# A weight matrix for each of the two dense blocks of a graph-attention layer, and the second block started three slots after the first

## The chip, the cores and the metric

The kernel runs on one core of one Trainium2 chip. A core has five engines that work through queues of their own: TensorE (PE in the profile; its weight loads are listed as PEld), VectorE (DVE), ScalarE (ACT), GpSimd (POOL) and SyncE (SP, which here only starts transfers). They meet through semaphores. The on-chip memory has 128 partitions; TensorE writes its products into a separate accumulator memory (PSUM). Transfers between the device's main memory and the on-chip memory run on 16 DMA engines that all queues share.

The metric is device time in microseconds (us) of one execution of the whole program; lower is better. The kernel before has a median of 2652.23 us over nine runs (2638.36 to 2659.0).

## The reference

One block of a graph network over 6250 nodes with 256 features and 100,000 edges, sorted by destination. Destinations are drawn with a square law, so that the low-numbered nodes have by far the most edges.

```python
xn = layernorm(x)
# graph layer 1 (GCN), with self loops
h1 = relu(segment_sum((xn @ W1)[src] * dinv[src] * dinv[dst], dst) + b1)
# graph layer 2 (GAT)
xw = h1 @ W2
e  = leaky_relu((xw @ a_src)[src] + (xw @ a_dst)[dst], 0.2)
p  = exp(e - segment_max(e, dst)[dst])
h2 = relu(segment_sum(p[:, None] * xw[src], dst) / segment_sum(p, dst) + b2)
x  = x + h2 + mix(xn)              # mix: linear attention with normed k and v
x  = x + experts(layernorm(x))     # two of eight experts a node, gelu between
```

The change lies in the second graph layer (the lines of `e`, `p` and `h2`).

## The kernel before, in words

Nodes are cut into 49 blocks of 128 (`NB = 49`, `P = 128`). The edges of a block of destinations are packed into tiles of 128 edges. For 47 of the blocks a tile's source rows are fetched from a table in main memory (`ftab`: 256 features, a one, the source's score and its parts, 260 numbers a row) by an indirect DMA of GpSimd, one gather for 128 rows, and are added up by TensorE with a matrix that has the edge's weight at (edge, destination). The first two blocks (`ND = 2`) have so many edges that they are done densely: `many[:, b, :, :]` holds how many edges run from each of the 6272 (padded) sources to each of the 128 destinations of block b, and the attention weight is worked out for every pair, in a matrix `W` of 128 x 49 x 128 numbers (24.5 KB a partition). TensorE then multiplies it with all of `ftab`, which is streamed through in 14 transfers of 900 KB (seven for each block) into two buffers `F`.

The second layer is written as a plan over slots. A slot is a third or a half of a chunk (8 to 12 tiles of one block). A chunk that begins at slot s is announced at s - 12, gathered from s - 14, its scores transposed, looked up and turned into weights by s - 1, and added up from slot s on. Slots before 0 are the start-up; the dense blocks are planned into them. For every slot the loop runs the lists `loads`, `early`, then the aggregation `add_up2` (line 1932), then `tensor`, then `late` and `last`. The order of TensorE, ScalarE, VectorE and GpSimd is exactly the order in which the loop issues; only SyncE's transfers are ordered by the scheduler. Every engine takes its instructions in order, so that one that waits holds up all behind it.

The gathered rows go into a ring of 75 rows. Its first 48 lie in the tile `xres`, the last 27 (`NR2 = 27`) in a tile of their own, `ring2` (named `ring` in the profile). A row can be filled again once TensorE has added up the tile that was in it. At the start all rows are empty, so that the first 75 gathers can run ahead.

The steps of a dense block b that is planned at slot s, by their lines in the kernel before:

- s, `seen`, lines 1993 (ScalarE) and 1994 (VectorE), seven times each: which sources are seen, and their scores, into W.
- s + 1, `tops`, line 1998 (VectorE): the maximum over the sources; s + 2, transposed by TensorE (2002), and `maxima` (2006 to 2015, VectorE, small).
- s + 3, `in_rows`, line 2019 (TensorE): the destinations' scores and maxima in rows.
- s + 4, `plus`, line 2022, and `leaky`, line 2027 (VectorE): the score and the leaky relu.
- s + 5, `minus`, line 2030 (VectorE), and `powers_of`, line 2041 (ScalarE): minus the maximum, and the exponential.
- s + 6, `times`, line 2045 (VectorE): times the number of edges.
- s + 7, `through`, line 2051 (TensorE): 49 matmuls with the streamed `F` (line 2036 starts the transfers).
- s + 8, `dense_taken`, line 2061 (VectorE): the block itself is added, into `dacc`.

In the kernel before the first block has s = -14 and the second s = -7, and both use the one W. After the second layer's slots the rest of the experts' work follows; part of it runs within the slots.

Of the kernel before, what the change touches and what calls it, by code (L numbers as in the profile page):

```python
# [9 lines left out]
FP = mybir.dt.float32  # L10
# [4 lines left out]
AF = mybir.ActivationFunctionType  # L15
ALU = mybir.AluOpType
AX = mybir.AxisListType
# [7 lines left out]
P = 128  # L25
# [9 lines left out]
def graph_block(  # L35
# [22 lines left out]
    nc = tc.nc  # L58
# [6 lines left out]
    NB = (N + P - 1) // P  # L65
# [36 lines left out]
    ND, GD, MOST = 2, 8, 2048  # L102
    GPB, HS = P // GD, 7
# [13 lines left out]
    GW = D + 4  # L117
# [55 lines left out]
    with ExitStack() as s0:  # L173
# [170 lines left out]
        for i in range(NB):  # L344
            st = e2.tile([P, 6], FP, name="st")
# [1024 lines left out]
    def roomy():  # L1370
# [14 lines left out]
        with ExitStack() as s1:  # L1385
# [116 lines left out]
        with ExitStack() as s2:  # L1502
# [24 lines left out]
            for b in range(ND, NB):  # L1527
# [186 lines left out]
        with ExitStack() as s3:  # L1714
# [30 lines left out]
            NR1, NR2 = NB * RW // GW, 27  # L1745
            NR3 = NR1 + NR2
            ring1 = xres.rearrange("p i d -> p (i d)")[:, : NR1 * GW].rearrange("p (i d) -> p i d", d=GW)
            ring2 = rp.tile([P, NR2, GW], FP, name="ring")
# [7 lines left out]
            GO = 14  # L1756
# [198 lines left out]
            def at(plan, s, what, *of):  # L1955
                plan.setdefault(s, []).append((what, of))

            for ch in chunks:
                s, n = ch["at"], len(ch["cut"]) - 1
# [22 lines left out]
                    at(late, s + n + 1, end, ch)  # L1982

            dm = tc.alloc_tile_pool(name="dm", bufs=1, side="right")
            W = dm.tile([P, NB, P], FP, name="W")
            pshares = ex.take()
            nc.scalar.copy(pshares[:, :NB], share[:, :, 0])
            shares = pshares[:, :NB, None]

            def seen(b, h0):  # L1990

                hs = slice(h0, h0 + HS)
                nc.scalar.activation(W[:, hs, :], many[:, b, hs, :], AF.Identity, bias=lowest, scale=BIG)
                nc.vector.tensor_tensor(W[:, hs, :], W[:, hs, :], shares[:, hs].to_broadcast([P, HS, P]), op=ALU.min)

            def tops(st):
                st["mx"] = mx = dm.tile([P, P], FP, name="mx")
                nc.vector.tensor_reduce(mx, W.rearrange("p h d -> p d h"), AX.X, ALU.max)

            def tops_turned(st):  # L2000
                st["pt"] = pt = ex.take()
# [17 lines left out]
                nc.tensor.matmul(pr, ones, st["diag"].rearrange("p j d -> p (j d)"), start=True, stop=True)  # L2019

            def plus(st):
                nc.vector.tensor_tensor(W, W, st["pr"][:, None, :P].to_broadcast([P, NB, P]), op=ALU.add)

            def leaky():
                for h0 in range(0, NB, HS):
                    part = W[:, h0 : h0 + HS, :]
                    nc.vector.scalar_tensor_tensor(part, part, 0.2, part, op0=ALU.mult, op1=ALU.max)

            def minus(st):
                nc.vector.tensor_tensor(W, W, st["pr"][:, None, P:].to_broadcast([P, NB, P]), op=ALU.subtract)  # L2030
                ex.give(st["pr"])
                nc.scalar.activation(st["keep"], st["keep"], AF.Exp)

# [3 lines left out]
                    F, ftab[h0 * P : (h0 + HS) * P, 0 : D + 1].rearrange("(h p) d -> p h d", p=P)  # L2037
                )

            def powers_of(h0):  # L2040
                nc.scalar.activation(W[:, h0 : h0 + HS, :], W[:, h0 : h0 + HS, :], AF.Exp)

            def times(b, h0):
                hs = slice(h0, h0 + HS)
                nc.vector.tensor_tensor(W[:, hs, :], W[:, hs, :], many[:, b, hs, :], op=ALU.mult)

            def through(st, h0):
                if h0 == 0:
                    st["pa"] = ps3.tile([P, D + 1], FP, name="agg", bufs=2)
                for h in range(h0, h0 + HS):  # L2050
                    nc.tensor.matmul(
                        st["pa"], W[:, h, :], st["F", h0][:, h - h0, :], start=(h == 0), stop=(h == NB - 1)
                    )

            def dense_own(b, st):
# [20 lines left out]
            nc.vector.tensor_scalar(lowest, lift, -1.0, None, op0=ALU.mult)  # L2076
            parts7 = range(0, NB, HS)
            for b in range(ND):
                st, s = {}, -GO + 7 * b
                for h0 in parts7:  # L2080
                    at(late, s, seen, b, h0)
                at(late, s + 1, tops, st)
                at(tensor, s + 2, tops_turned, st)
                at(late, s + 2, maxima, b, st)
                at(tensor, s + 3, in_rows, st)
                at(late, s + 4, plus, st)
                at(late, s + 4, leaky)
                at(late, s + 5, minus, st)
                at(loads, s + 2, dense_own, b, st)
                for n, h0 in enumerate(parts7):  # L2090
                    at(loads, s + 4 + n // 3, stream, st, h0)
                    at(last, s + 5, powers_of, h0)
                    at(late, s + 6, times, b, h0)
                    at(tensor, s + 7, through, st, h0)
                at(late, s + 8, dense_taken, b, st)
                at(loads, 3, dense_mixed, b, st)
                at(late, 4 + b, dense_end, b, st)
# [59 lines left out]
```

## Time and profile before

| what | value |
|---|---|
| median of nine runs | 2652.23 us (2638.36 to 2659.0) |
| profiled execution, its own time | 2645.85 us |
| its span | 2644.1 us |
| busy: PE, DVE, ACT, POOL | 1978.0, 1473.6, 756.6, 1593.2 us |
| start-up of the second layer (first `seen` to first regular aggregation after the dense blocks) | about 1149 to 1312 us |
| its regular slots | about 1312 to 2275 us |
| the experts' rest | about 2275 to 2644 us |

The page gives busy time by engine, the span in 40 slices, and the costliest groups of instructions. In a list in order of time a row has start, duration, engine, line, operation, what it writes and reads, its shape and how many instructions are merged; in brackets stands how long the engine was idle ahead of it, and what ended the wait. "issue" means that nothing the profile shows was waited for. A matmul of 32-bit numbers appears as two passes, so 49 matmuls are 98 passes. `x7` marks seven instructions merged into one row. The granted clock of TensorE is given as a share of full speed.

### The profile page before, as it was taken

The page shows a single profiled execution, that of the slowest core. Times are in us where ns is not written, and L with a number is a line of the kernel's source. Part 1 is how long each engine was busy: PE and PEld are TensorE (multiplying, and loading weights), DVE is VectorE, ACT ScalarE, POOL GpSimd, SP SyncE. Part 2 cuts the span into 40 slices and gives each one's busy share as a digit, 9 for nine tenths or more (in the row PEclk, how much of TensorE's full clock was granted, in tenths as well). Part 3 has the DMA queues.
Part 4 walks back from the last instruction along what each step waited for, and adds up shares of the span by engine and source line. Part 5 has one row for each costly group of instructions (what it writes and reads, how often), then busy time and mean ns, then how long its engine had stood idle before and what let it go on. Part 6 is the DMA issues. An engine that isn't in the chain of part 4 may idle for free. (4 is left out here: it accounts for less than half of the span.)

```text
span 2644.1 us, 34183 instructions
## 1 busy us (share of the span) xinstructions
PE 1978.0 (75%) x9261; PEld 1465.0 (55%) x9261; DVE 1473.6 (56%) x5122; ACT 756.6 (29%) x1914; POOL 1593.2 (60%) x1753
## 2 busy tenths in 40 slices
PE   3478888888889987734677679989998797688600
PEld 2355555555556666623445457767776585576500
DVE  6422454554534424476598676888776676531332
ACT  3242112232332200012233234544544353211100
POOL 1106777777777767747177777777777774100076
PEclk9698898988999989967799789999998898799855
DMA  4254344444447567746355576777676665364366
GB/s 135 56 189 149 114 119 120 122 122 121 126 131 225 161 207 221 219 137 209 115 172 165 148 232 204 224 238 228 210 241 210 212 192 160 100 231 151 119 200 177
DMA packets 299243, 450.28 MB, mean 170 GB/s; under 512 B 44666, under 2 KB 225566, under 8 KB 298879
## 3 DMA queue, kind: packets, MB, share of 16 engines
q0 software_dynamic: 77184, 210.12, 27.9%
q1 hardware_dynamic: 209710, 226.65, 26.8%
q10 hardware_dynamic: 12145, 11.19, 1.4%
q8 instruction: 78, 1.28, 0.2%
q14 instruction: 126, 1.03, 0.1%
HBM read 377.19 MB, written 71.40 MB: 170 GB/s over the span
## 5 line engine op out<-in xcount | busy, mean ns | idle before, releaser
L1576 POOL DMA_INDIRECT xres<-ytab,srcidx x698 | 688.8, 987 | 304.0 <-DMA wr<-in_L_mix_w_qkv_dram 82.8
L1798 POOL DMA_INDIRECT xres<-ftab,srcidx x455 | 450.3, 990 | 210.6 <-PE agg L1932 82.1
L1580 PE MATMUL agg<-xres,S 128*128 128x256 f32 x1396 | 380.9, 410 | 70.0 <-DMA xres<-ytab,srcidx 68.4
L1580 PEld LDWEIGHTS agg<-xres,S 128*128 128x128 f32 x1396 | 265.4, 200 | 181.1 <-DMA xres<-ytab,srcidx 126.8
L1798 POOL DMA_INDIRECT ring<-ftab,srcidx x243 | 237.6, 978 | 74.1 <-issue 27.1
L1932 PE MATMUL agg<-xres,PW 128*128 128x257 f32 x910 | 248.1, 415 | 11.8 <-ACT PW L1925 11.8
L880 PE MATMUL px<-xT,w1q 128*128 128x256 f32 x896 | 231.1, 410 | 29.2 <-DVE xT L868 14.9
L1925 ACT ACTIVATE PW<-S,z 128x128 f32<-128x128 bf16 x698 | 224.5, 392 | 98.9 <-DVE S L1908 32.3
L956 POOL DMA_INDIRECT yg<-ys,part x98 | 96.7, 987 | 229.3 <-issue 215.0
L880 PEld LDWEIGHTS px<-xT,w1q 128*128 128x128 f32 x896 | 175.7, 204 | 63.2 <-DVE xT L868 18.1
L902 PE MATMUL px<-w2q,hT 128*128 128x256 f32 x896 | 208.1, 383 | 1.1 <-DVE yb L907 1.0
L434 DVE TENSOR_REDUCE var<-sq 128x16 f32<-128x1024 f32 x49 | 59.8, 1220 | 260.6 <-ACT sq L432 260.6
L1932 PEld LDWEIGHTS agg<-xres,PW 128*128 128x128 f32 x910 | 180.4, 206 | 41.0 <-ACT PW L1925 12.8
L427 PE MATMUL kv<-wkvT,xnT 128*128 128x512 f32 x392 | 182.2, 608 | 8.8 <-DVE vv L446 8.8
L902 PEld LDWEIGHTS px<-w2q,hT 128*128 128x128 f32 x896 | 166.5, 190 | 25.3 <-DVE yb L907 1.4
L887 ACT ACTIVATE hT<-px,b1T 128x256 f32<-128x256 f32 x224 | 96.1, 472 | 231.3 <-PE px L880 194.9
L784 POOL DMA_INDIRECT xs<-xn,to_i x98 | 99.9, 1019 | 101.5 <-DVE slot L761 63.0
L907 DVE TENSOR_TENSOR yb<-px,fb 128x256 f32<-128x256 f32 x112 | 44.7, 421 | 198.0 <-PE px L902 170.1
L1932 PE MATMUL agg<-ring,PW 128*128 128x257 f32 x486 | 133.0, 416 | 0.0
L427 PEld LDWEIGHTS kv<-wkvT,xnT 128*128 128x128 f32 x392 | 76.0, 199 | 88.5 <-issue 74.3
L1844 DVE TENSOR_REDUCE mt<-pm 128x1 f32<-128x384 f32 (+1 forms) x201 | 122.2, 608 | 1.5 <-PE pm L1837 1.5
L1908 DVE TENSOR_TENSOR S<-iota_b,dlc 128x384 bf16<-128x384 bf16 (+1 forms) x201 | 122.9, 612 | 0.0
(359 smaller groups left out, 3210.3 us busy)
## 6 DMA issues: line engine op xcount, KB each, us to landing
w1q<-in_L_ffn_W_dram SPq DMA_DIRECT2D x56, 512.0 KB
w2q<-in_L_ffn_W_dram SPq DMA_DIRECT2D x56, 512.0 KB
xg<-xs SPq DMA_DIRECT2D x56, 256.0 KB
ys<-yb SPq DMA_DIRECT2D x56, 256.0 KB
F<-ftab SPq DMA_DIRECT2D x14, 899.5 KB
Y<-ytab SPq DMA_DIRECT2D x14, 896.0 KB
xnT<-xnTd SPq DMA_DIRECT2D x98, 128.0 KB
xres<-ytab,srcidx POOLq DMA_INDIRECT x698
```

Of the source, the lines that this page charges most:

```text
L427: nc.tensor.matmul(kv[:, s, :], xnT[:, k, :], wkvT[:, k, s * INNER : (s + 1) * INNER], start=(k == 0), stop=(k == 1),)
L784: put = nc.gpsimd.indirect_dma_start(out=xs[:, :], out_offset=bass.IndirectOffsetOnAxis(ap=to_i[:n, j, k : k + 1], axis=0), in_=bt["xn"][k ...
L880: nc.tensor.matmul(ph, w1q[:, k, c * P : (c + 1) * P], xT[:, k, :], start=(k == 0), stop=(k == 1))
L902: nc.tensor.matmul(py, hT[:, c, j * P : (j + 1) * P], w2q[:, c, :], start=(c == 0), stop=(c == HC - 1))
L956: back = nc.gpsimd.indirect_dma_start(out=yg[:n, :], out_offset=None, in_=ys[:, :], in_offset=bass.IndirectOffsetOnAxis(ap=self.slot[:n, j ...
L1576: nc.gpsimd.indirect_dma_start(out=R, out_offset=None, in_=ytab[:, :], in_offset=bass.IndirectOffsetOnAxis(ap=srcidx[:, t : t + 1], axis=0),)
L1580: nc.tensor.matmul(sums[b], hot[s][:, t - t0, :], R, start=(t == first[b]), stop=(t == first[b + 1] - 1))
L1798: nc.gpsimd.indirect_dma_start(out=ch["R"][c], out_offset=None, in_=ftab[:, :], in_offset=bass.IndirectOffsetOnAxis(ap=srcidx[:, ch["t0"] ...
L1844: nc.vector.tensor_reduce(ch["mt"][:, q : q + 1], ch["pm", q][:, :w, :].rearrange("p c e -> p (c e)"), AX.X, ALU.max)
L1908: nc.vector.tensor_tensor(S[:, : c1 - c0], iota_b[:, None, :].to_broadcast([P, c1 - c0, P]), dlc[:, t0 + c0 : t0 + c1, None].to_broadcast( ...
L1925: nc.scalar.mul(PW[:, c - c0, :], ch["S", q][:, c - c0, :], ch["z"][:, c : c + 1])
L1932: nc.tensor.matmul(ch["pa"], ch["PW", q][:, c - c0, :], ch["R"][c][:, 0 : D + 1], start=(c == 0), stop=(c == ch["C"] - 1),)
```

## The change

Each dense block has a weight matrix of its own. The first block's is laid over the first 6272 of the 7020 numbers (a partition) of the ring's last 27 rows, `ring2`; the second block's is the tile `W` that was there. The ring's gathers into those rows follow in the program behind the first block's use of them. The second block is planned three slots behind the first (s = -11) and no longer seven (s = -7). The steps, their operations and their shapes are the same; the functions take the block's state `st`, from which they read its matrix.

```diff
             dm = tc.alloc_tile_pool(name="dm", bufs=1, side="right")
-            W = dm.tile([P, NB, P], FP, name="W")
+
+            assert NR2 * GW >= NB * P and ND == 2
+            Ws = [
+                ring2.rearrange("p i d -> p (i d)")[:, : NB * P].rearrange("p (h d) -> p h d", d=P),
+                dm.tile([P, NB, P], FP, name="W"),
+            ]
...
-            def seen(b, h0):
-
-                hs = slice(h0, h0 + HS)
+            def seen(b, st, h0):
+
+                W, hs = st["W"], slice(h0, h0 + HS)
...
             def plus(st):
-                nc.vector.tensor_tensor(W, W, st["pr"][:, None, :P].to_broadcast([P, NB, P]), op=ALU.add)
-
-            def leaky():
+                nc.vector.tensor_tensor(st["W"], st["W"], st["pr"][:, None, :P].to_broadcast([P, NB, P]), op=ALU.add)
+
+            def leaky(st):
                 for h0 in range(0, NB, HS):
-                    part = W[:, h0 : h0 + HS, :]
+                    part = st["W"][:, h0 : h0 + HS, :]
                     nc.vector.scalar_tensor_tensor(part, part, 0.2, part, op0=ALU.mult, op1=ALU.max)
...
                 for h in range(h0, h0 + HS):
                     nc.tensor.matmul(
-                        st["pa"], W[:, h, :], st["F", h0][:, h - h0, :], start=(h == 0), stop=(h == NB - 1)
+                        st["pa"], st["W"][:, h, :], st["F", h0][:, h - h0, :], start=(h == 0), stop=(h == NB - 1)
                     )
...
             for b in range(ND):
-                st, s = {}, -GO + 7 * b
+                st, s = {"W": Ws[b]}, -GO + 3 * b
                 for h0 in parts7:
-                    at(late, s, seen, b, h0)
+                    at(late, s, seen, b, st, h0)
                 at(late, s + 1, tops, st)
...
                 at(late, s + 4, plus, st)
-                at(late, s + 4, leaky)
+                at(late, s + 4, leaky, st)
                 at(late, s + 5, minus, st)
```

`tops`, `minus`, `powers_of` and `times` read `st["W"]` in the same way.

More of the change, by code (lines that the diff above doesn't have):

```diff
@@ L1997, in tops @@
                 st["mx"] = mx = dm.tile([P, P], FP, name="mx")
-                nc.vector.tensor_reduce(mx, W.rearrange("p h d -> p d h"), AX.X, ALU.max)
+                nc.vector.tensor_reduce(mx, st["W"].rearrange("p h d -> p d h"), AX.X, ALU.max)
             def tops_turned(st):
@@ L2021, in plus @@
             def plus(st):
-                nc.vector.tensor_tensor(W, W, st["pr"][:, None, :P].to_broadcast([P, NB, P]), op=ALU.add)
-            def leaky():
+                nc.vector.tensor_tensor(st["W"], st["W"], st["pr"][:, None, :P].to_broadcast([P, NB, P]), op=ALU.add)
+            def leaky(st):
                 for h0 in range(0, NB, HS):
-                    part = W[:, h0 : h0 + HS, :]
+                    part = st["W"][:, h0 : h0 + HS, :]
                     nc.vector.scalar_tensor_tensor(part, part, 0.2, part, op0=ALU.mult, op1=ALU.max)
             def minus(st):
-                nc.vector.tensor_tensor(W, W, st["pr"][:, None, P:].to_broadcast([P, NB, P]), op=ALU.subtract)
+                nc.vector.tensor_tensor(st["W"], st["W"], st["pr"][:, None, P:].to_broadcast([P, NB, P]), op=ALU.subtract)
                 ex.give(st["pr"])
@@ L2038, in stream, with powers_of, times @@
                 )
[L2040 to L2044, printed above, removed]
+            def powers_of(st, h0):
+                part = st["W"][:, h0 : h0 + HS, :]
+                nc.scalar.activation(part, part, AF.Exp)
+            def times(b, st, h0):
+                W, hs = st["W"], slice(h0, h0 + HS)
                 nc.vector.tensor_tensor(W[:, hs, :], W[:, hs, :], many[:, b, hs, :], op=ALU.mult)
@@ L2091, in roomy @@
                     at(loads, s + 4 + n // 3, stream, st, h0)
-                    at(last, s + 5, powers_of, h0)
-                    at(late, s + 6, times, b, h0)
+                    at(last, s + 5, powers_of, st, h0)
+                    at(late, s + 6, times, b, st, h0)
                     at(tensor, s + 7, through, st, h0)
```

## The prediction

> **What bounds the kernel now.** I read the page first (shares, slices, costliest groups), then the busy time by stage, then GpSimd's, VectorE's and TensorE's instructions in order of time around the start of the second layer, and last the waits.
>
> Lines of the costliest groups: all of the second layer's gathers are issued by GpSimd at line 1798, 455 + 243 = 698 of them.
>
> ```profile
> L1798 POOL DMA_INDIRECT xres<-ftab,srcidx x455 | 450.3, 990 | 210.6 <-PE agg L1932 82.1
> L1798 POOL DMA_INDIRECT ring<-ftab,srcidx x243 | 237.6, 978 | 74.1 <-issue 27.1
> ```
>
> Busy time by stage (columns: PE, PEld, DVE, ACT, POOL with instruction counts, granted clock, DMA share, GB/s):
>
> ```profile
> 1250.00:1270.00 20.00, 1.20 (x6) 0.44 (x5) 19.97 (x11) 0.00 (x0) 1.86 (x2) 0.50 0.08 20
> 1290.00:1310.00 20.00, 16.18 (x59) 12.94 (x58) 0.00 (x0) 0.00 (x0) 0.00 (x0) 0.83 0.54 162
> 1500.00:1600.00 100.00, 79.09 (x439) 61.47 (x436) 66.61 (x283) 39.68 (x120) 76.23 (x79) 0.86 0.65 203
> 1800.00:1900.00 100.00, 94.65 (x541) 75.00 (x540) 82.90 (x342) 47.60 (x143) 76.18 (x79) 0.95 0.76 241
> ```
>
> From 1400 to 2200 us GpSimd does 78 or 79 instructions in every 100 us, whatever the others do. In its list one gather starts 1.253 us after the last (0.95 busy, 0.30 between), and 100/1.253 is 79.8: it is saturated, so it paces the layer. From 1312.8 us to its last gather (2223.1) no idle of more than 0.31 us stands before a gather. The two long ones are earlier:
>
> ```profile
> 1251.22 0.95 POOL L1798 DMA_INDIRECT ring<-ftab,srcidx  x1 [0.31 <-issue]
> 1278.28 2.91 POOL L1798 DMA_INDIRECT xres<-ftab,srcidx  x1 [26.11 <-PE agg L1932]
> 1312.80 1.11 POOL L1798 DMA_INDIRECT xres<-ftab,srcidx  x1 [27.60 <-PE agg L1932]
> ```
>
> The ring has 75 rows. At 1252 us all are full, and gather 76 needs the first aggregation (line 1932) to free a row. That comes late because VectorE and TensorE are still at the dense blocks:
>
> ```profile
> 1157.21 10.62 DVE L1998 TENSOR_REDUCE mx<-W 128x128 f32<-128x6272 f32 x1
> 1228.93 1.09 DVE L1994 TENSOR_TENSOR W<-W,px 128x896 f32<-128x896 f32 x1 [3.81 <-ACT W L1993]
> 1232.53 10.62 DVE L1998 TENSOR_REDUCE mx<-W 128x128 f32<-128x6272 f32 x1
> 1263.73 6.68 DVE L2030 TENSOR_TENSOR W<-W,px 128x6272 f32<-128x6272 f32 x1
> 1312.13 0.48 DVE L2061 SCALAR_TENSOR_TENSOR dacc<-own,dkeep,agg 128x257 f32<-128x257 f32 x1 [28.54 <-PE agg L2051]
> ```
>
> Block 1's first pass (line 1994) creeps from 1200.9 to 1230.0 us because each seventh of the one W is rewritten only after block 0's products have read it; its other passes follow only then. TensorE's products (line 2051) themselves wait for F:
>
> ```profile
> 1194.02 8.24 PE L2051 MATMUL agg<-F,W 128*128 128x257 f32 x28 [6.29 <-DVE W L2045]
> 1224.54 3.28 PE L2051 MATMUL agg<-F,W 128*128 128x257 f32 x14 [1.62 <-DMA F<-ftab]
> 1280.62 6.36 PE L2051 MATMUL agg<-F,W 128*128 128x257 f32 x28
> 1308.81 3.28 PE L2051 MATMUL agg<-F,W 128*128 128x257 f32 x14 [1.88 <-DMA F<-ftab]
> ```
>
> Block 0's products take 1194.0 to 1227.8 = 33.8 us, block 1's 1280.6 to 1312.1 = 31.5 us: 4.8 and 4.5 us per seventh, against 3.28 for a seventh's matmuls at full clock. So: what the change is worth is how much earlier gather 80 starts (1312.80 now), since from it on GpSimd runs without a pause.
>
> **The change part by part.** All durations are from the profiled execution (2645.85 us, span 2644.1), 6.4 us under the median of the nine runs (2652.23); I apply the difference to the median.
>
> *Nothing is added or removed.* The same passes, matmuls, 14 F loads and gathers run; only places in the queues change. Two places are checked for a new wait below.
>
> *VectorE's chain to block 0's products.* By the built order block 1's first pass (7.1) and its maximum (10.62) now stand between block 0's steps. Up to 1169.7 (diagonals of block 0) nothing moves. Then: first pass of block 1 7.1, to 1176.8 (its ScalarE half no longer waits for products; the 1.31 wait for line 2019 is hidden beneath it); line 2022 6.7, to 1183.5; line 2027 7.1, to 1190.6; block 1's maximum 10.6, to 1201.2; Q 0.4 and line 2030 6.7, to 1208.3; block 1's small steps 1.3, to 1209.6; first seventh of line 2045 1.1, to 1210.7. TensorE must first do block 1's row product (1.22) and a pm group (0.59 + 0.60) after 1209.6, so block 0's products start at 1212.1, not 1194.0: 18.1 us later. With 33.8 us they end at 1245.9.
>
> *Block 1's chain.* Lines 2022 and 2027 of block 1 (13.8) run beneath block 0's products, 1218 to 1232. But line 2030 of block 1 stands behind block 0's dacc (line 2061) on VectorE, so it waits for 1245.9: dacc 0.5 and line 2030 6.7, to 1253.1; then 2.2 to TensorE's first matmul (before: line 2030 ended 1191.9, products began 1194.0), so 1255.3. Queued behind dacc are also the pm reduction that TensorE needs ahead of the products (0.55, beneath the exponential) and Q of the third chunk, for which SP's dq load stands ahead of four F loads: Q ends near 1262, when the F buffer of the second seventh is read (1255.3 + 6.4), so SP loses about nothing. Block 1's first two F come as block 0's last buffers free (1241 and 1246) and land before 1255.3, as they were ahead at 1280.6 before. With 31.5 us the products end at 1286.8, not 1312.1.
>
> A row bounds this span from the other side: the 33.8 of block 0, whose first 28 matmuls took 8.24 at granted clock 0.5 instead of 6.36. TensorE will have done little for 9 us before. The Trainium skill, "TensorE: Matmul & The Clock Gate" (What's actually happening), has the clock fall to half after an idle window of about 3.4 us; the 8.24 after an idle of 6.29 agrees, and by that rule the sum below would be about 2 us worse.
>
> *From there to a free row.* Now slots -3 to -1 stand between. dacc 0.5 and the one-hot S 0.7 to 1288.0; pm reduction 0.55 and a pm group 0.8 on TensorE to 1289.3, beneath which ScalarE's four scalings run (1.27); a row is free 1.5 after the aggregation starts (1276.78 to 1278.28): gather 76 at 1290.8, gather 80 four periods (5.0) later, 1295.8. Ends: 0.7 for all of it (1312.1 to 1312.80 before), or 4 us more if the slots' small steps do not overlap, and 2 more if gather 76 again lasts 2.91.
>
> *Ring rows hold block 0's W.* The built order shows each of gathers 49 to 72 now waiting for TensorE on its own. Row r needs W's columns up to about 2.03(r + 1); with block 0's sevenths read from 1212.1 to 1245.9, row 9 is free at 1227 (nominal start 1229.9), row 23 at 1246 (1247.5): nearly no wait. Even if all 27 waited for 1245.9 they would end 27 x 1.253 = 33.8 us later, at 1279.7, still 11 us under gather 76. I take nothing. The cover is gone if block 0's products end after 1257.
>
> *After gather 80.* Everything is paced by GpSimd. ScalarE still waits 24.0 us for gathers at the very end:
>
> ```profile
> 2214.98 0.23 ACT L1808 COPY a<-xres 128x44 bf16<-128x44 bf16 x1 [16.17 <-DMA xres<-ftab,srcidx]
> 2226.03 0.23 ACT L1808 COPY a<-xres 128x44 bf16<-128x44 bf16 x1 [7.83 <-DMA xres<-ftab,srcidx]
> ```
>
> so the shift reaches the end of the layer, and the experts behind it hold the same work in the same order.
>
> Sum: 1312.8 - 1295.8 = 17.0 us. Ends: 17.0 + 3.0 = 20 (gather 76 0.7 after the products), and 17.0 - 2.3 - 4 - 2 = 8.7. I take 17.0: its terms are rows of this very stretch. Profiled: 2628.9; against the median: 2635.
>
> **The rivals.**
> *The loads get dearer (slower).* The F loads share the DMA engines with the gathers: from 1210 to 1230 their busy share is 0.96 at 293 GB/s. With A and B the two product spans, gather 80 starts at 1230.5 + A + B; it breaks even at A + B = 82.3, or 5.9 us per seventh for all 14, and is 0.3% slower from 6.5. The dearest row is the F load issued at 1202.3 whose matmuls started at 1210.5 (8.2). At 6.6 per seventh, 10 us slower: 2662. For it: that share. Against: block 0's 4.8 were already beside gathers, and they end near 1255 as before, so block 1's are not. In the Trainium skill, "DMA: Bandwidth & Descriptors" (Issuing engines are not separate DMA queues) says that queues of different engines do not bring separate DMA engines; 293 GB/s with both streams against 162 with F alone shows that one stream alone left room here.
>
> *The gain is swallowed (same).* TensorE is 94% busy from 1800 to 2000 us, and there ScalarE hardly waits for gathers; were TensorE the true pacer with GpSimd only keeping up, an earlier start would be lost in between: 2652. Against: before 1600 ScalarE waits for gathers over and over (some 80 us from 1400 to 1600), and again at the end, so TensorE's own work would start earlier too.
>
> *More is saved.* If F were always there in time for block 1, its products would take 7 x 3.28 = 23 us, 8.5 less: 2627. Against: two buffers, and a load of about 5 us (issued 1283.96, used 1288.98).
>
> **How the numbers follow.** Forecast 0.72 (2632 to 2644 by its own ends), more saved 0.06, swallowed 0.12, dearer loads 0.10. What a measurement of this kernel can tell from no change is about 0.3%, 8 us; all of the forecast lies beyond it. So faster 0.78, same 0.12, slower 0.10. The nine runs spread over 21 us, so a median may be off by some 3. The range takes in most of "more saved" and half of "swallowed": 2626 to 2651.
>
> **What would show it.** After: block 1's first pass in one piece at about 1170; block 0's products from 1212 to 1246; dacc of block 0 with a wait of some 12 us ahead of it; block 1's products from 1255 to 1287; one long idle before gather 76, ending near 1291, in place of 26.1 and 27.6; no other above 3 us; last gather near 2206. Wrong if the products' spans sum to over 70 us, if a gather after 76 waits for TensorE again, or if the last gather is early but the span is not.

## The result and the profile after

The changed kernel takes **2629.13 us** (median of ten runs, 2622.86 to 2637.31), the kernel before beside it 2651.87 us (31 runs, 2638.36 to 2659.3). The ratio is 0.9918, with a 95% interval of 0.9903 to 0.9933: 22.7 us by the medians. The forecast was 2635 us, in a range from 2626 to 2651.

The profiled execution of the changed kernel is not a typical one: 2640.6 us (span 2638.8), 11.5 us above its median. The excess lies ahead of everything that the change touches: the dense blocks' first pass on VectorE (line 1999, `seen`, 1994 before) starts at 1161.67 us, in the profile before at 1150.10, and in a second profile of the changed kernel, which lies at its median, at 1153.12. All offsets below are therefore counted from that pass in each profile. "Gather n" is the n-th of the second layer's gathers (line 1798); the two columns of the changed kernel are its first profile and the one of a second group of runs. In the lists, rows that lie between those shown are left out.

| us after the first dense pass | before | forecast | after | after, again |
|---|---|---|---|---|
| block 0's products | 43.9 to 77.7 | 62.0 to 95.8 | 61.5 to 94.9 | 61.4 to 96.7 |
| block 1's products | 130.5 to 162.0 | 105.2 to 136.7 | 104.2 to 134.9 | 106.0 to 136.1 |
| gather 76 | 128.2 | 140.7 | 138.1 | 139.3 |
| gather 80 | 162.7 | 145.7 | 143.3 | 144.5 |
| last gather | 1073.0 | 1055.9 | 1058.4 | 1055.2 |
| from gather 80 to the end of the span | 1331.3 | 1331.3 | 1333.9 | 1335.0 |
| from the first dense pass to the end of the span | 1494.0 | 1477.0 | 1477.1 | 1479.5 |

By the last line the profiles differ by 16.9 and 14.5 us. Of what gather 80 gained, 2.6 and 3.7 us are lost behind it, and 5.8 of the 22.7 us by the medians are not seen behind the first dense pass of the first profile.

Gather 76 comes 9.9 us later than before, and gather 80 comes 19.4 us earlier. GpSimd's instructions of the changed kernel in order of time show how both can be:

```profile
1266.94 1.70 POOL L1798 DMA_INDIRECT ring<-ftab,srcidx  x1 [0.31 <-issue]
1299.79 0.95 POOL L1798 DMA_INDIRECT xres<-ftab,srcidx  x1 [31.16 <-PE agg L1932]
1301.05 0.95 POOL L1798 DMA_INDIRECT xres<-ftab,srcidx  x1 [0.31 <-PE agg L1932]
1302.30 0.95 POOL L1798 DMA_INDIRECT xres<-ftab,srcidx  x1 [0.30 <-PE agg L1932]
1303.56 1.07 POOL L1798 DMA_INDIRECT xres<-ftab,srcidx  x1 [0.30 <-PE small L1881]
1304.93 1.09 POOL L1798 DMA_INDIRECT xres<-ftab,srcidx  x1 [0.31 <-DVE S L1908]
```

The first row is gather 75, which fills the last row of the ring; the last is gather 80. One idle of 31.16 us stands in place of the two of 26.11 and 27.60. Behind it no gather of the layer has an idle of even 0.6 us ahead of it. In the costliest groups of the page the idle before the `xres` gathers falls from 210.6 to 190.0 us, which is 20.6; the `ring` gathers, into rows that the first block's W now holds, have 74.1 as before:

```profile
L1798 POOL DMA_INDIRECT xres<-ftab,srcidx x455 | 452.0, 993 | 190.0 <-issue 77.7
L1798 POOL DMA_INDIRECT ring<-ftab,srcidx x243 | 243.2, 1001 | 74.1 <-issue 20.7
```

VectorE's rows of the same profile show where block 1's work went. Its first pass stands in one piece (7.07 us for seven instructions, before spread over 29 us), 19.6 us behind block 0's first, and its maximum comes ahead of block 0's last pass, the multiplication (2051):

```profile
1181.31 7.07 DVE L1999 TENSOR_TENSOR W<-W,px 128x896 f32<-128x896 f32 x7
1202.03 10.61 DVE L2003 TENSOR_REDUCE mx<-W 128x128 f32<-128x6272 f32 x1
1220.95 7.09 DVE L2051 TENSOR_TENSOR ring<-ring,many 128x896 f32<-128x896 f32 x7
1256.62 0.48 DVE L2067 SCALAR_TENSOR_TENSOR dacc<-own,dkeep,agg 128x257 f32<-128x257 f32 x1 [11.60 <-PE agg L2057]
1257.02 6.68 DVE L2035 TENSOR_TENSOR W<-W,px 128x6272 f32<-128x6272 f32 x1
1264.72 7.11 DVE L2051 TENSOR_TENSOR W<-W,many 128x896 f32<-128x896 f32 x7 [0.55 <-ACT W L2047]
```

The names tell the blocks apart: `ring` is the matrix of block 0, `W` that of block 1. The 11.60 ahead of `dacc` is the one wait that the new order brings to VectorE; block 1's subtraction of the maximum (2035) stands right behind it.

TensorE's products (line 2057), in the same profile:

```profile
1223.20 8.52 PE L2057 MATMUL agg<-F,ring 128*128 128x257 f32 x28
1253.30 3.28 PE L2057 MATMUL agg<-F,ring 128*128 128x257 f32 x14 [1.47 <-DMA F<-ftab]
1265.87 9.36 PE L2057 MATMUL agg<-F,W 128*128 128x257 f32 x28 [0.74 <-DVE W L2051]
1277.00 3.28 PE L2057 MATMUL agg<-F,W 128*128 128x257 f32 x14 [1.77 <-DMA F<-ftab]
1293.26 3.28 PE L2057 MATMUL agg<-F,W 128*128 128x257 f32 x14 [1.14 <-DMA F<-ftab]
```

From the end of one block's products to the start of the other's there are 9.3 us now (1256.6 to 1265.87), where there were 52.8.

### The profile page after: what moved, and what is told of

Its sections match the earlier page's. It is cut to its first block, busy times and chain, and to the rows that moved or that the text cites. A ratio compares the mean times of both kernels' runs of the same rounds, so it can differ in the third digit from the quotient of the medians.

```text
span 2638.8 us, 34197 instructions
## 1 busy us (share of the span) xinstructions
PE 1992.6 (76%) x9261; PEld 1471.9 (56%) x9261; DVE 1472.6 (56%) x5122; ACT 755.5 (29%) x1914; POOL 1605.5 (61%) x1753
## 5 line engine op out<-in xcount | busy, mean ns | idle before, releaser
L1798 POOL DMA_INDIRECT xres<-ftab,srcidx x455 | 452.0, 993 | 190.0 <-issue 77.7
L1580 PE MATMUL agg<-xres,S 128*128 128x256 f32 x1396 | 387.4, 415 | 71.4 <-DMA xres<-ytab,srcidx 69.7
L1798 POOL DMA_INDIRECT ring<-ftab,srcidx x243 | 243.2, 1001 | 74.1 <-issue 20.7
L1932 PE MATMUL agg<-xres,PW 128*128 128x257 f32 x910 | 257.4, 427 | 0.0
```

The lines of the kernel that those rows point to most:

```text
L1580: nc.tensor.matmul(sums[b], hot[s][:, t - t0, :], R, start=(t == first[b]), stop=(t == first[b + 1] - 1))
L1798: nc.gpsimd.indirect_dma_start(out=ch["R"][c], out_offset=None, in_=ftab[:, :], in_offset=bass.IndirectOffsetOnAxis(ap=srcidx[:, ch["t0"] ...
L1932: nc.tensor.matmul(ch["pa"], ch["PW", q][:, c - c0, :], ch["R"][c][:, 0 : D + 1], start=(c == 0), stop=(c == ch["C"] - 1),)
```

## The experiments

The theory: all that counts is when gather 80 starts, from which on GpSimd runs without a pause; it comes earlier because block 1's passes no longer wait for block 0's products, and each microsecond of it reaches the end. The rivals: the second matrix alone does it, whatever the slots; or the gain is in part swallowed later; or the end follows something else than gather 80. The first group of runs, on one chip with the kernel before at 2653.18 us (23 runs), tells these apart.

### The changed kernel again

> The changed kernel once more, with a second profile. Theory (the second layer is paced by GpSimd from gather 80 on, so the whole time moves with the start of that gather): measured from the first pass of block 0 on VectorE, gather 80 starts about 143 us later as in the first profile of the changed kernel (before: 162.7), and from there to the end of the span it takes the same as before, 1331 us, within some 5. If the part of the gain above the forecast 17 us came from after gather 80, this last stretch would be some 5 us shorter than before in both profiles.

Measured: 2634.69 us, ratio 0.994 (0.9922 to 0.9957), with its offsets in the table above. Gather 80 came 18.2 us ahead of the profile before and the median is 18.5 us lower. It is the reference for the other three of this group.

### Two matrices, but seven slots

```diff
-                st, s = {"W": Ws[b]}, -GO + 3 * b
+                st, s = {"W": Ws[b]}, -GO + 7 * b
```

> Two matrices, but the second block again seven slots behind the first. Theory: block 1's first pass no longer waits for block 0's products, but its maximum stands on VectorE behind block 0's dacc, which waits for the end of those products; so block 1's maximum starts only about 4 us earlier than before (1228.6 in place of 1232.5 on the clock of the profile before), and the time falls by about 4 us, to 2648. Rival (the separate matrix alone is what helps): about 2629, like the changed kernel.

Measured: 2648.18 us, ratio 0.9986 (0.997 to 1.0002). Block 0's products at 44.0 to 79.2, block 1's at 128.4 to 161.4, gather 80 at 162.1. GpSimd's two long idles are back:

```profile
1273.44 2.90 POOL L1798 DMA_INDIRECT xres<-ftab,srcidx  x1 [23.21 <-PE agg L1932]
1310.08 1.10 POOL L1798 DMA_INDIRECT xres<-ftab,srcidx  x1 [29.75 <-PE agg L1932]
```

Block 1's first pass does stand in one piece here too, since it has a matrix of its own, and yet its products begin only 2.1 us sooner than before. VectorE's rows show why: block 1's maximum stands behind block 0's `dacc`, and that waits for block 0's products.

```profile
1227.24 0.48 DVE L2067 SCALAR_TENSOR_TENSOR dacc<-own,dkeep,agg 128x257 f32<-128x257 f32 x1 [18.97 <-PE agg L2057]
1227.64 10.61 DVE L2003 TENSOR_REDUCE mx<-W 128x128 f32<-128x6272 f32 x1
```

The maximum comes 2.8 us sooner than before, where 4 were expected (79.6 us after the first dense pass instead of 82.4). The second matrix by itself is worth little or nothing; it is what allows the three slots, and those carry the gain.

### Block 1's products twice

Every matmul of block 1 is repeated into a spare accumulator that nobody reads; the output stays as it was. This makes only TensorE's stretch longer.

```diff
                     nc.tensor.matmul(
                         st["pa"], st["W"][:, h, :], st["F", h0][:, h - h0, :], start=(h == 0), stop=(h == NB - 1)
                     )
+                if st["W"] is Ws[1]:
+                    px = ex.take()
+                    for h in range(h0, h0 + HS):
+                        nc.tensor.matmul(px, st["W"][:, h, :], st["F", h0][:, h - h0, :D], start=True, stop=True)
+                    ex.give(px)
```

> The changed kernel with block 1's 49 products done twice, the second time into a spare accumulator (the output stays the same). Theory: a seventh then takes 2 x 3.28 = 6.6 us of TensorE in place of 4.4 with its wait for F, so the products take some 46 us in place of 30.7, gather 76 starts 15 us later, and the time rises by the same 15 us, to 2644. Rival (the start of the gathers is not what the end follows; there is slack behind it): 2629 to 2634.

Measured: 2646.46 us, ratio 0.9985 (0.9972 to 0.9997). With the repeats the products take 45.3 us (105.2 to 150.5) against 30.1 in the run beside it; gather 80 starts at 158.4, 13.9 later, and the median is 11.8 later (the means differ by 12.1, give or take 4.0). So a delay at this place comes out at the end almost whole. The 15 us expected was 3 too many by the medians, less than the scatter. TensorE's rows also show that the loads are hidden once it has two passes for each seventh; the row of the repeats (line 2063) and the next seventh follow without an idle:

```profile
1253.36 5.87 PE L2057 MATMUL agg<-F,W 128*128 128x257 f32 x14 [0.73 <-DVE W L2051]
1259.07 3.19 PE L2063 MATMUL px<-F,W 128*128 128x256 f32 x14
1262.09 3.21 PE L2057 MATMUL agg<-F,W 128*128 128x257 f32 x14
1265.14 3.19 PE L2063 MATMUL px<-F,W 128*128 128x256 f32 x14
```

### Block 1's products spread over slots

In the changed kernel all seven parts of block 1's products stand in one slot, ahead of the first regular aggregation that frees a row. Here two stay there, and the other five go into the next five slots, one each; `dacc` of block 1 follows them. (The text on record for the last group says six parts in one slot each; it is five.)

```diff
-                    at(tensor, s + 7, through, st, h0)
-                at(late, s + 8, dense_taken, b, st)
+                    at(tensor, s + 7 + b * max(0, n - 1), through, st, h0)
+                at(late, s + (12 if b else 8), dense_taken, b, st)
```

> The changed kernel with block 1's products spread over six slots: two sevenths in slot -4, one in each of the slots -3 to 1, and dacc of block 1 in slot 1. Theory: gather 76 waits for the aggregation of slot 0, which on TensorE now stands behind five sevenths and no longer behind all seven; so gather 76 starts about 10 us earlier (some 127 us after block 0's first pass, not 138) and the time falls by 8 to 10 us, to about 2620. Rival (the end follows the end of the dense products, wherever the aggregations stand): 2629.

Measured: **2622.07 us**, ratio 0.9894 (0.9873 to 0.9915), 12.6 us under the changed kernel beside it (means 13.0, give or take 6.2). Gather 80 comes at 132.8, 11.7 us sooner. TensorE's rows show the aggregation (line 1932) between the parts, ahead of the last two, and GpSimd's first idle ended by it:

```profile
1275.37 3.31 PE L2057 MATMUL agg<-F,W 128*128 128x257 f32 x14 [0.31 <-DMA F<-ftab]
1278.52 1.90 PE L1932 MATMUL agg<-xres,PW 128*128 128x257 f32 x8
1280.77 3.31 PE L2057 MATMUL agg<-F,W 128*128 128x257 f32 x14
```

```profile
1279.38 0.94 POOL L1798 DMA_INDIRECT xres<-ftab,srcidx  x1 [20.87 <-PE agg L1932]
```

With these four and the two profiles of the beginning, gather 80 lies anywhere from 132.8 to 162.7, and the stretch from it to the end only from 1330.6 to 1335.0. That is the theory's claim, and the rival of a gain swallowed later falls with it. So do two other places that the end might follow: block 1's products end 1.8 us later in the spread run than in the changed one beside it (137.9 and 136.1), and its first regular aggregation starts where that of the kernel before does (126.5 and 126.7).

One reading does not fit as well. The stretch from gather 80 to the last gather is not constant: it takes 910.3 to 918.7 us in these six profiles, longest in the spread run, whose last gather comes only 3.7 us sooner than in the run beside it (1051.5 and 1055.2). What is left behind the last gather, 412.0 to 424.3 us, makes up for it there. So it is shown that the end follows gather 80 within some 4 us; that it follows GpSimd's last gather as closely is not shown.

### Where the wait for `dacc` matters

The next two groups ran on other chips, where the kernel before takes 3193.04 and 3188.77 us, so that their times are compared only with each other and with the kernel before of the same group. The question is the 9.3 us between the two blocks' products, which the prediction put down to `dacc` waiting on VectorE ahead of block 1's subtraction (2035; one of the expectations calls it the scaling). Here block 0's `dacc` goes one slot later and behind block 1's passes of that slot:

```diff
-                at(late, s + 8, dense_taken, b, st)
+                at(late, s + (8 if b else 9), dense_taken, b, st)
...
+            late[-GO + 9].sort(key=lambda t: t[0] is dense_taken)
```

> The changed kernel with one instruction moved: dacc of block 0 stands on VectorE behind block 1's last pass (line 2051) and no longer ahead of its subtraction. Theory: block 1's subtraction then runs beneath block 0's products, and block 1's products start some 2.5 us after block 0's end, not 9 to 10; F then limits them, and the transfer of a later block's own rows that waits for dacc stands ahead of block 1's third F, so that their end and gather 76 come 4 to 7 us earlier, and the time is 4 to 7 us under the changed kernel's. Rival (F alone sets when block 1's products end, so that the wait on VectorE costs nothing): the changed kernel's time.

Measured: 3130.83 us, ratio 0.9802 (0.9772 to 0.9831); products at 61.4 to 99.0 and 107.1 to 137.8, gather 80 at 146.1. Block 1's products were expected 2.5 us behind block 0's and come 8.1 behind them. VectorE's small reduction of the regular slots (line 1844), which stands ahead of block 1's last pass, starts 6.4 us after block 0's products end; "remote" stands where the profile names nothing of this core that ended the wait, and what did stays open:

```profile
1473.36 0.56 DVE L1844 TENSOR_REDUCE mt<-pm 128x1 f32<-128x384 f32 x1 [15.68 <-remote]
```

The changed kernel itself was not in this group; the spread kernel with the same edit was:

> The spread products and the moved dacc of block 0 together. Theory (end = start of gather 80 + 1331 to 1335 us): block 1's products start about 6 us earlier than with the spread alone, gather 80 starts near 127 us after block 0's first pass (spread alone 132.8), and the time is some 5 us under that of the spread alone, about 30 to 35 us under the kernel before. Rival (behind the spread other steps of the slots limit gather 76): no different from the spread alone.

Measured: 3125.66 us, ratio 0.9791 (0.9766 to 0.9817), products at 61.4 to 100.6 and 105.2 to 138.7, gather 80 at 133.6, where some 127 was expected. The gain over the kernel before is 67 us by the medians, not 30 to 35. By these two alone it could not be said what the moved `dacc` gives. The last group had the changed kernel, the spread one, and the spread one with `dacc` moved on one chip:

> The changed kernel again, as the reference for the three beside it. Gather 80 at 143 to 145 us after the first dense pass on VectorE and 1330 to 1335 us from it to the end; some 0.6 to 0.8% under before. If the runs show otherwise, the comparisons of the other three go by this run and not by the earlier one.

> The changed kernel with six of block 1's seven part products put into one slot each, so that aggregations stand between them. My theory (each us that gather 80 comes earlier reaches the end): gather 80 at 133, 11 to 12 us ahead of the changed kernel's, and the time 0.4 to 0.5% under the changed kernel's beside it. Rival (the earlier gain of 12.6 us was in part the scatter between runs): 0.1 to 0.2% under, though gather 80 comes as early.

> The same with block 0's dacc behind block 1's scaling pass on VectorE as well. Theory: the dacc's wait of some 12 us lies beside block 0's products, and TensorE's two products cannot be nearer than the F loads allow (products 1 started 105 to 107 after the first dense pass with or without this on the other chip), so gather 80 comes within 2 us of the spread kernel's and the time is the same within 0.15%. Rival (the wait for dacc holds block 1's scaling and so its products): products 1 start 5 to 8 us sooner, at 97 to 100, gather 80 at 125 to 128, and the time is 0.2 to 0.3% under the spread kernel's.

| | median, us | ratio to before | block 0's products | block 1's products | gather 80 |
|---|---|---|---|---|---|
| changed | 3141.71 | 0.9836 (0.9802 to 0.9869) | 61.5 to 100.2 | 112.7 to 147.6 | 156.0 |
| spread | 3132.5 | 0.9818 (0.9788 to 0.9848) | 61.4 to 101.8 | 113.2 to 146.0 | 140.9 |
| spread, `dacc` moved | 3116.55 | 0.9777 (0.9747 to 0.9807) | 61.4 to 103.5 | 106.9 to 139.5 | 134.4 |

The changed kernel's gather 80 was expected at 143 to 145 and came at 156.0: on this chip its products take 38.7 and 34.9 us, and 12.5 us lie between them. Of the 12.5, the last 9.24 are the same as on the first chip, and 3.26 lie ahead of `dacc`, where the profile names no cause. Its gain over before is larger here, 47 us by the medians, 1.5% where 0.6 to 0.8% was expected; why was not settled, as there is no profile of the kernel before from that chip. The spread alone gives 9.2 us (expected 0.4 to 0.5%, got 0.3%, and the means' 6.8, give or take 8.4, do not exclude that it gives nothing); on the first chip it was clear.

With `dacc` moved as well my theory expected no change within 0.15%, and that was wrong: 16 us less by the medians (means 13.6, give or take 6.1), gather 80 6.5 us sooner. Block 1's products begin 3.4 us behind block 0's (103.5 to 106.9) instead of 11.4 (101.8 to 113.2). The rival was right in its cause and in the 5 to 8 us by which they start sooner (6.3 against the spread kernel), while the places it named (97 to 100 for the products, 125 to 128 for gather 80) were too early, and the gain in time was twice the one it gave. Gather 80 accounts for 6.5 us of that gain; another 7.3 lie behind it in the two profiles (1620.2 and 1612.9 us to the end) and are not explained. VectorE's rows of the spread kernel, then of the one with `dacc` moved, show the order and why the products don't start sooner still:

```profile
1471.84 0.48 DVE L2067 SCALAR_TENSOR_TENSOR dacc<-own,dkeep,agg 128x257 f32<-128x257 f32 x1 [20.73 <-PE small L1881]
1472.23 6.68 DVE L2035 TENSOR_TENSOR W<-W,px 128x6272 f32<-128x6272 f32 x1
```

```profile
1448.38 6.68 DVE L2035 TENSOR_TENSOR W<-W,px 128x6272 f32<-128x6272 f32 x1
1470.57 0.56 DVE L1844 TENSOR_REDUCE mt<-pm 128x1 f32<-128x384 f32 x1 [15.51 <-PE small L1881]
1471.04 7.09 DVE L2051 TENSOR_TENSOR W<-W,many 128x896 f32<-128x896 f32 x7
```

Block 1's subtraction now runs early, in the shade of block 0's products. But a small reduction of the regular slots (1844), which needs a lookup that stands behind block 0's products on TensorE, takes over the wait: 15.51 us. Only when it is done can the last pass (2051) run. So the wait of 11.60 us in the changed kernel was no idle that costs nothing: what stood behind it, 6.68 us and the steps to TensorE, lay on the path. The profiles of all three chips agree on its price: from the start of `dacc` to block 1's products there are 9.24 or 9.25 us in all eight with three slots and `dacc` in its old place, and in the three with `dacc` moved there are 1.61 us from the reduction to them.

### A gap of four slots

```diff
-                st, s = {"W": Ws[b]}, -GO + 3 * b
+                st, s = {"W": Ws[b]}, -GO + 4 * b
```

> The changed kernel with the second block four slots behind the first, not three. By the order on VectorE block 0's chain is as long as with three (block 1's first pass and maximum stand in it), but block 1's addition and leaky relu (13.8 us) now stand behind block 0's dacc, which waits for the end of block 0's products, and no longer ahead of it. Theory: block 1's products start some 14 us later than with three, near 119 us after block 0's first pass, gather 80 near 158, and the time is 13 to 15 us above the changed kernel's, some 4 under the kernel before. Rival (any overlap of the two blocks gives the gain; the number of slots matters little): the changed kernel's time.

Measured, in the first of the two later groups: 3160.06 us, ratio 0.9892 (0.9875 to 0.9908). Products at 60.9 to 104.1 and 132.1 to 166.3, gather 80 at 173.6, where block 1's products were expected near 119 and gather 80 near 158. The changed kernel was not in this group, so the 13 to 15 us between the two kernels could not be read. VectorE's rows, and one of TensorE, say what the fourth slot of the gap costs:

```profile
1466.08 0.48 DVE L2067 SCALAR_TENSOR_TENSOR dacc<-own,dkeep,agg 128x257 f32<-128x257 f32 x1 [33.12 <-issue]
1466.51 6.69 DVE L2027 TENSOR_TENSOR W<-W,px 128x6272 f32<-128x6272 f32 x1
1473.23 7.10 DVE L2032 SCALAR_TENSOR_TENSOR W<-W 128x896 f32<-128x896 f32 x7
1480.72 6.67 DVE L2035 TENSOR_TENSOR W<-W,px 128x6272 f32<-128x6272 f32 x1
1465.88 0.59 PE L2024 MATMUL px<-diag,ones 128*128 128x256 f32 x2
```

With four slots block 1's other two passes (2027 and 2032, 13.8 us) have fallen behind `dacc` too, and `dacc` waits 33.12 us while VectorE has nothing else to do. (The row names no releaser, but block 0's products end at 1466.0, just as it starts.) The last row is something that was not expected: block 1's row product (`in_rows`), which its pass 2027 reads, now also stands behind block 0's products on TensorE, so that 2027 could not have run sooner even without `dacc` ahead of it. Between the two blocks' products lie 28.0 us. So what a slot costs is read from which instructions fall behind block 0's products, on VectorE and on TensorE; gaps of five and six slots were not tried.

### The two matrices exchanged

The prediction costed the ring rows that block 0's matrix holds at nothing, because its sevenths are read in time. Here block 1's matrix, read later, lies in these rows.

```diff
-                st, s = {"W": Ws[b]}, -GO + 3 * b
+                st, s = {"W": Ws[1 - b]}, -GO + 3 * b
```

It was run in both of the later groups.

> The changed kernel with the two matrices exchanged: block 0 has the tile of its own, block 1 lies in the ring's last 27 rows. Gathers 49 to 75 then wait for block 1's products, which end some 135 us after block 0's first pass. Theory (gathers that are done before gather 76 can start cost nothing): the 27 gathers follow the products row by row and end near 138 us, where gather 76 would start anyway, so the time is that of the changed kernel, at most 3 us more. Rival (work taken from GpSimd's early stretch must be made up later, 27 x 1.253 us): 30 us or more above the changed kernel, slower than the kernel before.

> The changed kernel with the two W exchanged: block 1's in the ring's last rows, block 0's apart. Theory as the prediction had it (ring rows held by a W cost nothing while the products end before the first free row): gather 49 is held to about 110 and the rows behind it to the end of block 1's products near 136, so gathers 49 to 75 are issued late and gather 76 can come no sooner than some 27 x 1.25 us after the first of them is let go. Held row by row, gather 75 ends up near 149 and gather 80 near 157, as on the other chip, 12 to 14 us behind the changed kernel's, and the time is 0.45 to 0.55% above the changed kernel's. Rival (rows are freed at random places, GpSimd catches up out of the slack later): gather 80 as late, but the time within 0.15% of the changed kernel's.

Measured: 3146.01 us (ratio 0.9858, 0.9835 to 0.9882), and beside the changed kernel 3144.04 us (0.9855, 0.9825 to 0.9885), 2.3 us above it by the medians (means 6.3, give or take 9.0, so neither nothing nor the 0.45% of the theory's lower end is excluded). Gather 49, the first into these rows, is held for 41.80 and 44.42 us, and gather 80 comes at 157.4 and 159.4. In the first of the two runs the theory missed: gather 75 was expected near 138 and came at 148.7. The expectation of the second was drawn up after that. GpSimd's rows of the second run, gathers 49, 75 and 76:

```profile
1488.98 1.56 POOL L1798 DMA_INDIRECT ring<-ftab,srcidx  x1 [44.42 <-PE agg L2057]
...
1527.28 0.95 POOL L1798 DMA_INDIRECT ring<-ftab,srcidx  x1 [0.30 <-issue]
1529.97 0.94 POOL L1798 DMA_INDIRECT xres<-ftab,srcidx  x1 [1.75 <-PE agg L1932]
```

There the place was as forecast: gather 75 at 151.7, and gather 76 right behind it. Gather 80 is only 3.4 us late against the changed kernel of this chip, because that one's own was at 156.0. The rival of 30 us or more is out. So a held ring can cost something, as the prediction's condition had it (free if the products end early enough), but here the hold ends when the products do, and little is left. How much it would cost on the first chip was not tried.

## Why the prediction was right, point by point

What was forecast stands in bold, what the runs showed behind it.

- **GpSimd paces the layer from gather 80 on, and the end follows it 1:1.** Shown: from gather 80 to the end there are 1330.6 to 1335.0 us in six profiles, while gather 80 moves over 30 us, and behind it GpSimd has no idle of 0.6 us ahead of any gather (1.99 in the spread run). The rival of a gain swallowed in TensorE's busy stretch is out for this chip. That GpSimd is what carries the shift to the end is the best reading of these idles, but it is argued: on the slower chips the end follows gather 80 too, though GpSimd waits there.
- **Block 0's products 18.1 us later.** 61.5 for 62.0, and 33.4 us long for 33.8 (35.3 in the second profile). Block 1's first pass was forecast 19.6 behind the first dense pass and came at 19.6.
- **`dacc` waits some 12 us, and block 1's products start 9.4 behind block 0's.** 11.60 and 9.3. That this gap is made by `dacc`'s place was shown by moving it, on a slower chip: 11.4 became 3.4.
- **Block 1's products take 31.5 us.** 30.7, by a mix that I had not foreseen. Their first 28 matmuls took 9.36 us, not 6.36, and TensorE's granted clock in that window was 0.70 of full speed (columns: PE, PEld, DVE, ACT, POOL, then clock, DMA share and GB/s):

```profile
1256.60:1265.80 9.20, 2.31 (x21) 1.04 (x20) 8.63 (x5) 2.06 (x3) 7.07 (x8) 0.78 0.80 253
1265.80:1276.00 10.20, 9.36 (x28) 7.33 (x28) 9.58 (x24) 4.51 (x9) 2.53 (x2) 0.70 0.40 116
1276.00:1297.00 21.00, 16.86 (x77) 13.21 (x78) 0.42 (x2) 0.00 (x0) 0.00 (x0) 1.00 0.64 196
```

  So the rule of the Trainium skill, "TensorE: Matmul & The Clock Gate" (What's actually happening), that the clock is at half after an idle window of about 3.4 us, fits these matmuls: an idle of 6.22 us lay just ahead, and they were 3.0 us dearer. (The prediction gives the 8.24 us of block 0's first 28 matmuls in the kernel before a granted clock of 0.5. That is the clock just ahead of them; over the 8.3 us of the matmuls, 1194.0 to 1202.3, it was 0.77.) But the span did not grow by it, since the other five sevenths took 19.6 us, 115.3 to 134.9, instead of 23.1 before. Why those were quicker was not settled.
- **Gather 76 4.0 behind the products, gather 80 5.0 behind it.** 3.2 and 5.1.
- **Held ring rows cost nothing.** In the changed kernel, on the first chip, gathers 49 to 75 have 0.30 or 0.31 us of idle ahead, though several are released by line 2057. The exchange shows that this is a matter of the order of reading, not of the matrix lying there.
- **The rival of dearer F loads.** The two product spans, the prediction's A + B, took 64.1 us together, far from the 82.3 at which the change would break even. Even on a slower chip, where they took 73.6, the change gained.
- **The rival of more saved (2627 us).** The time came out near that rival's, but not by its cause: it had F always there and block 1's products in 23 us. They took 30.7, and TensorE still waits for F ahead of most sevenths.
- **The size.** The sum gave 17.0 and gather 80 moved 19.4. The 2.4 us are made of the start of block 1's products (1.0 sooner), their length (0.8 shorter) and the step to gather 76 (0.8 shorter), less 0.1 from there to gather 80. No step failed. By the medians the gain was 22.7 (17.8 to 25.7 by the interval's ends) and, in the second group, 18.5. From the first dense pass to the end the profiles gained 16.9 and 14.5, so that the working accounts for the smaller figures, and the rest of the 22.7 is not explained by it. Two terms of the forecast's own ends are loose: gather 76 at 0.7 instead of 4.0 behind the products gives 3.3, not 3.0, and the 2.3 of the lower end has no row beside it; the slow matmuls above, which it may stand for, left the span as it was.

## What to carry to other kernels

Look for the instruction that waits for another engine's long stretch, and list what stands behind it in its queue: whatever could have run under that stretch is the price. Giving a buffer to each of two overlapping jobs gave next to nothing here until the order was changed to use it, and the order is best judged by which instructions fall behind such a wait, on every engine, not by a distance in slots. Where a ring of buffers paces the rest, a job that stands ahead of the first instruction that frees a row should be cut into parts with that instruction between them.

## What was not expected of the hardware

**Gathers slowed by some of VectorE's passes.** Beside most work a gather takes 0.95 us and the next starts 1.25 after it. Beside two of the passes it takes some 1.70 and the next starts 2.00 after it. GpSimd's and then VectorE's rows of the changed kernel:

```profile
1193.82 0.95 POOL L1798 DMA_INDIRECT xres<-ftab,srcidx  x1 [0.30 <-issue]
1195.08 1.84 POOL L1798 DMA_INDIRECT xres<-ftab,srcidx  x1 [0.31 <-issue]
1197.23 1.70 POOL L1798 DMA_INDIRECT xres<-ftab,srcidx  x1 [0.30 <-issue]
1199.23 1.70 POOL L1798 DMA_INDIRECT xres<-ftab,srcidx  x1 [0.30 <-issue]
1201.23 1.70 POOL L1798 DMA_INDIRECT xres<-ftab,srcidx  x1 [0.30 <-issue]
1203.24 0.95 POOL L1798 DMA_INDIRECT xres<-ftab,srcidx  x1 [0.30 <-issue]
```

```profile
1188.29 6.68 DVE L2027 TENSOR_TENSOR ring<-ring,px 128x6272 f32<-128x6272 f32 x1
1195.01 7.10 DVE L2032 SCALAR_TENSOR_TENSOR ring<-ring 128x896 f32<-128x896 f32 x7
1202.03 10.61 DVE L2003 TENSOR_REDUCE mx<-W 128x128 f32<-128x6272 f32 x1
```

The slow ones begin and end with line 2032 (the same is seen beside line 2051), and 2.00 us are two of its instructions (seven in 7.10). Those two lines read both inputs from the on-chip memory; line 2027, which leaves the gathers at 0.95, has its second input `px` in the accumulator memory, and line 2003 has one input. The Trainium skill, "SBUF — State Buffer" (Who interferes with whom), says that a VectorE instruction with two inputs in that memory contends with a GpSimd instruction that reads it. The trace agrees with which lines slow the gathers; a gather was delayed by about 0.75 us here, and not for the whole pass, which is seven instructions; whether it waits for one of them to end is not shown. The changed kernel puts more such passes ahead of gather 75, which comes 105.3 us after the first dense pass instead of 101.1. It cost nothing, as gather 76 waited for TensorE for another 31.16 us.

**One program, two speeds by chip.** The kernel before took 2653.18 us on the chip of the first group, 3193.04 and 3188.77 on those of the later ones. The busy times are nearly the same (changed kernel, first and third group: VectorE 1473.4 and 1470.4 us, GpSimd 1597.4 and 1591.5), so on these two engines the difference is idle time between instructions; TensorE is busy 93.5 us longer (2076.0 against 1982.5), at a mean granted clock of 0.814 instead of 0.874. On the chip of the third group GpSimd does 57 to 68 instructions in 100 us of the regular slots (1600 to 2600 us) instead of 78, and it waits for free rows again. Yet over the eight profiles of the two slow chips the stretch from gather 80 to the end is 1612.9 to 1625.9 us, while gather 80 moves over 40 us. There the earlier start goes through to the end, within some 13 us, although GpSimd is not busy without a pause; why was not looked into.
